# A fused two-layer convolution block: one xs store for each unit of layer 0, another buffer for a chunk of layer 1's results, three steps moved in the written order

## The chip, the core and the metric

The kernel runs on one core of a Trainium2 chip. It uses the core's five engines, named here as in the profile: PE (TensorE: matmuls, with its weight loads PEld), DVE (VectorE), ACT (ScalarE), POOL (GpSimd) and SP (SyncE, which here only issues DMAs), and 16 DMA engines. "ACTq" and "SPq" mark the DMAs and semaphore waits that ACT and SP take from their instruction queues. The metric is the device time of one execution in microseconds (us), the median of several.

## What is computed

Input x has 4 batches of 64 channels, 256 by 256, in float32. Two layers follow each other, each on a group-normalised input and with its input added:

```python
# --- layer 0 ---
h  = conv3x3(gn(x), c1_w) + c1_b
xa, k = split(conv1x1(h, c2_w) + c2_b, 2, axis=1)
xs = gelu(conv_vertical(conv_horizontal(xa, sh_w) + sh_b, sv_w) + sv_b)   # depthwise, 3 taps each
mask = top2(softmax(mean(xs, (2, 3)) @ gate_w.T))
out = xs
for i in range(3):                       # low ranks 2, 4, 8
    e = conv1x1(conv1x1(k, w2[i]) * conv1x1(xs, w1[i]), w3[i])
    out = out + e * mask[:, i]
x = x + conv1x1(out, proj_w)
# --- layer 1 ---
g = gn(x)
h = relu(batchnorm(conv3x3(g, quantize(w1))))
h = batchnorm(conv3x3(h, quantize(w2)))
x = x + relu(h + g)
```

The mean of xs over a whole batch is needed before any output of layer 0 of that batch; the group norm of layer 1 needs the whole batch of layer 0's result y; the batch norms need all four batches.

## The kernel before

**Tiles.** A batch is cut into 16 chunks of 16 image rows; a chunk of one tensor is a tile of 128 partitions by 2048 float32 (8 KB in each partition, 1 MB). Results that don't fit into the on-chip memory go to DRAM and come back: xs (`xs_d`), the low-rank products (`low_d`), y (`y_d`), layer 1's first convolution h1 (`h1_d`). Buffers are tags with a number of copies; a new tile of a tag waits until the tile that had its copy is no longer used by any engine or DMA, and this is tracked for a tile as a whole.

**Stages**, as the profile shows them: statistics of batch 0 (0 to 100 us); the "front" of layer 0, 64 units, one for each chunk of each batch (100 to 1262 us), with the outputs of the batch before and the statistics of the batch after mixed in; the boundary (about 1250 to 1340); conv1 of layer 1, 4 batches of 16 chunks (to about 1960), with the outputs of layer 0's last ten half-chunks of batch 2 and of all of batch 3 in between; conv2 (to about 2500); the last addition (to the end).

**The order** of instructions is written out by hand. Each call is placed with `at(step, order, ...)`; the calls are sorted by step and, within a step, by order, and all five engines keep to it: an engine works through its own instructions in this order, and different engines meet only at semaphores. So a call that is moved matters where it passes another call's instruction on the same engine's queue. Unit u of the front has two steps, 2u and 2u+1 (`at_slot(u, pos, ...)`: a position below 6 lies in the first, from 6 on in the second). conv1 begins at step 128 (`CONV1`), chunk k of batch b is around step 128 + 65 b + 4 k. The work of units 62 and 63 that would fall past step 127 is placed among conv1's first steps by a table `TAIL`.

**A unit of the front.** After the 3x3 convolution of a unit, each of its two halves (sub 0 and 1) passes the taps: PE (`front_taps_a`, `front_taps_b`, ps_a at L513), ACT (`front_taps_i`, t at L699), DVE (`front_taps_h`, t at L706, L714, L717), then ACT's Gelu into an xs tile (`front_xs`, L730). ACT's queue issues the store of that half (`xs_store`, L735, 0.5 MB, rows of 4 KB). The xs tag has 4 copies of a half. Once for every two units PE multiplies their four halves by the experts' first weights (`front_q`, L766), DVE forms the low-rank product (`front_low`, L771, tile k) and SP stores it (`low_store`, low_d<-k).

**The outputs of layer 0.** xs and the low-rank products come back (`xs_load`, `low_load`), x comes as the tile y (`out_load`, L835, y<-in_xp), PE projects (`out_open`, ps_o), DVE adds in place (`out_add`, L880), SP stores (`out_store`, L893, y_d<-y). In conv1's time these are placed by `plan_out_late`.

**A chunk of conv1.** SP loads y with one row of the chunk above (`conv1_load`, L912, yn<-y_d). POOL takes differences of rows, half by half, into a tile d (`conv1_differences`, the helper at L343). ACT normalises odd rows (`conv1_upper_odd`, L930 and L359) and makes the upper parts (`conv1_upper`, L346), DVE the lower parts (`conv1_lower`, L353, and `conv1_lower_odd`, L362), both into tiles that PE convolves (ps_hm, then ps_h for g = 0 and 1, L296, 12 matmuls each). ACT makes the part m that both halves share (`conv1_shared`, L312; for k of 2 and more in the single copy of the tag "k", that of the low-rank product). DVE combines ps_h and m into h1 (`conv1_out`, L318; two halves g). ACT squares for the statistics (`conv1_square`, L382) and its queue stores h1 (L998, h_d<-h, 1 MB). The h1 of odd chunks goes into the tile that held x of the front ("x", one copy, `chunk_x`), that of even ones into "h1" (one copy); in batch 0 chunk 1 goes into "h1" too.

Of the kernel before, what the change touches and what calls it, by code (L numbers as in the profile page):

```python
# [9 lines left out]
F32 = mybir.dt.float32  # L10
# [9 lines left out]
P = 128  # L20
# [6 lines left out]
GF = GP * W  # L27
# [14 lines left out]
def conv_preact_kernel(ctx: ExitStack, tc: tile.TileContext, io, col128, colset, col64):  # L42
# [130 lines left out]

    def weights():

        m64_t = work.tile([P, 2, GF], F32, tag="xs", name="m64", bufs=4)
        m64 = flat(m64_t)[0:C, 0 : io["m64"].shape[1]]
        n = io["mc1"].shape[1]
        taps = flat(work.tile([P, 2 * GP, W], F32, tag="t", name="taps", bufs=1))[:, 0:n]
        nc.sync.dma_start(taps, io["mc1"])  # L180
        nc.sync.dma_start(m64, io["m64"])
        nc.sync.dma_start(m128, io["m128"])

        def c64(name):
            return m64[:, col64[name][0] : col64[name][1]]

        front_weights(taps)
        n = 9 * C
        nc.vector.tensor_tensor(flat(av), taps[:, n : n + 3 * C], taps[:, n + 3 * C : n + 6 * C], ALU.mult)

        nc.vector.tensor_reduce(sv_sum, c128("sv"), AX.X, ALU.add)
        nc.vector.tensor_reduce(sh_sum, sh, AX.X, ALU.add)
        nc.vector.tensor_scalar(sh_bias, sh_sum, c128("c2_ba"), c128("sh_b"), ALU.mult, ALU.add)
        nc.vector.tensor_scalar(tap_bias, sv_sum, sh_bias, c128("sv_b"), ALU.mult, ALU.add)
        for i in range(2):
            nc.vector.tensor_scalar(end[:, i : i + 1], sh[:, 2 * i : 2 * i + 1], c128("c2_ba"), None, ALU.mult)
        nc.vector.tensor_scalar(ends, end, sv_sum, None, ALU.mult)
        nc.vector.tensor_scalar(edge_bias, ends, -1.0, tap_bias, ALU.mult, ALU.add)
        for i in range(2):
            o = outer[:, i, :]  # L200
            nc.vector.tensor_scalar(o, zeros[:, 0:W], sh_bias, None, ALU.add)
            nc.vector.tensor_tensor(o[:, 0 : W : W - 1], o[:, 0 : W : W - 1], end, ALU.subtract)
            nc.vector.tensor_scalar(o, o, c128("sv")[:, 2 * i : 2 * i + 1], None, ALU.mult)

        nc.vector.memset(wk, 0.0)
        ps = small("ps_wk")
        nc.tensor.matmul(ps[:, 0:NLOW], c64("c2_k"), c64("w2_t")[:, 0:NLOW], start=True, stop=True)

        for s in range(2):
            half = slice(s * C, s * C + C)  # L210
            for i in range(2):
                o = 16 * i
                nc.vector.tensor_copy(wk[half, s, i, o : o + NLOW], ps[half, 0:NLOW])
        ps = small("ps_kb")
        nc.tensor.matmul(ps[:, 0:1], c64("w2_t"), c64("c2_bk"), start=True, stop=True)
        nc.vector.tensor_tensor(k_bias, ps[:, 0:1], c128("e_b2"), ALU.add)
        ps = small("ps_pw3")
        nc.tensor.matmul(ps[:, 0:C], c64("w3"), c64("proj_t")[:, 0:C], start=True, stop=True)
        nc.vector.tensor_copy(pw3, ps[:, 0:C])
        ps = small("ps_pb3")  # L220
        nc.tensor.matmul(ps[:, 0:3], c64("proj_t"), c64("b3"), start=True, stop=True)
        nc.vector.tensor_copy(pb3, ps[:, 0:3])
# [503 lines left out]
    def front_xs(u, sub):  # L726
        b, k = divmod(u, NCH)
        n = 2 * k + sub
        x = xss[b, n] = work.tile([P, 2, GF], F32, tag="xs", name=f"xs_{b}_{n}", bufs=4)
        nc.scalar.activation(flat(x), flat(open_t.pop((u, sub))), AF.Gelu, accum_out=pooled[b][:, n : n + 1])  # L730

    def xs_store(u, sub):
        b, k = divmod(u, NCH)
        n = 2 * k + sub
        nc.scalar.dma_start(xs_d[b][:, n, :], flat(xss[b, n]))  # L735

    def front_k(b, j):

# [21 lines left out]
    def front_q(b, j):  # L760

        ps = ps_q[b, j] = bank("p", f"ps_q_{b}_{j}").rearrange("p s a b -> p s (a b)")
        for s in range(2):
            for i in range(4):
                x = xss[b, 4 * j + i][:, s]
                nc.tensor.matmul(ps[32 * i : 32 * i + 32, s], c128("e_w1"), x, start=True, stop=True)  # L766

    def front_low(b, j):
# [145 lines left out]
    def conv1_differences(b, k):  # L914

        y = y_in[b, k]
        if k == 0:
            nc.gpsimd.tensor_scalar(y[:, 0, :], zeros[:, 0:W], gn2[b][:, 0:1], None, ALU.add)
        if b == 0 and k < 4:
            both_raw = chunk_out(f"d_{b}_{k}", "o", 2)  # L920
        for n in range(2):
            if b == 0 and k < 4:
                raw_in[b, k, n] = both_raw[:, 4 * n : 4 * n + 4, :]
            else:
                raw_in[b, k, n] = work.tile([P, 4, W], F32, tag="xs", name=f"d_{b}_{k}_{n}", bufs=4)
            differences(first_rows(y)[n], raw_in[b, k, n], nc.gpsimd)

    def conv1_upper_odd(b, k):
# [38 lines left out]

    def conv1_out(b, k, g):
        if g == 0:
            if k % 2 and (b > 0 or k > 2):  # L970
                h_out[b, k] = flat(chunk_x(f"h1_{b}_{k}"))[:, 0 : CPAIR * W].rearrange("p (a b) -> p a b", b=W)
            else:
                h_out[b, k] = conv1_pool[0].tile([P, CPAIR, W], F32, tag="h1", name=f"h1_{b}_{k}", bufs=1)
        h = h_out[b, k]
        at_h = h[:, 4 * g : 4 * g + 4, :]
        first = k == g == 0
        total = sums[b][:, 2 * k + g : 2 * k + g + 1]
        leave(at_h, open_h.pop((b, k, g)), m_in[b, k][:, g], "w1", None if first else total)
        if first:
            nc.vector.tensor_reduce(total, h[:, 1:4, :], AX.XY, ALU.add)  # L980
            nc.vector.tensor_reduce(sums[b][0:C, NOCT : NOCT + 1], h[0:C, 0, :], AX.X, ALU.add)
            if b == 0:
                totals_less("h1", h[:, 1:3, :])
        if g:
            del m_in[b, k]
# [71 lines left out]
    def at_each(places, chain):  # L1057
# [6 lines left out]
    SLOTS = UNITS + 3  # L1064

    TAIL = {
# [6 lines left out]
    }  # L1073
# [9 lines left out]
    def plan_front():  # L1083
# [4 lines left out]
        for u in range(SLOTS):  # L1088
# [26 lines left out]
            if 0 <= u - 2 <= last:  # L1115
                at_slot(u, 2, front_taps_a, u - 2, 1)
                at_slot(u, 2.2, divide, u)
                at_slot(u, 4, front_taps_b, u - 2, 1)
                at_slot(u, 4.15, front_taps_i, u - 2, 1)
                at_slot(u, 5.2, front_taps_h, u - 2, 1)  # L1120
                at_slot(u, 5.3, front_xs, u - 2, 1)
                at_slot(u, 6.135, xs_store, u - 2, 1)
            if 0 <= u - 1 <= last:
                at_slot(u, 7, front_taps_a, u - 1, 0)
                at_slot(u, 7.2, divide, u)
                at_slot(u, 9, front_taps_b, u - 1, 0)
                at_slot(u, 9.1, front_taps_i, u - 1, 0)
                at_slot(u + 1, 1.15, front_taps_h, u - 1, 0)
                at_slot(u + 1, 1.55, front_xs, u - 1, 0)
                at_slot(u + 1, 1.6, xs_store, u - 1, 0)  # L1130
            j = (u - 2) // 2
            if u % 2 == 0 and 0 <= j < UNITS // 2:
                at_slot(u, 8, front_k, *divmod(j, NOCT // 4))
# [72 lines left out]
    def plan_out_late(b, ns, steps, order, end):  # L1206

        for n, step in zip(ns, steps):
            if n % 2 == 0:
                at(step - 9, 0.2, low_load, b, n // 2)  # L1210
                at(step - 9, 0.3, xs_load, b, n // 2, "h")
                at(step - 6, 0.4, out_load, b, n // 2)
            at(step, order, out_slot, b, n)
            if n % 2:
                at(step + 1, 13.3, out_store, b, n // 2)
        at_each(end, out_end(b))

    def conv1_first():
# [12 lines left out]
    def plan_conv1(b):  # L1231
# [4 lines left out]
        for k in range(NCH):  # L1236
# [11 lines left out]
            at(load, 0, conv1_load, b, k)  # L1248
            at(*late(diff, 13.08), conv1_differences, b, k)
            at(*late(odd, 13.36 if b == 0 and k == 3 else 13.1), conv1_upper_odd, b, k)  # L1250
            at(*late(up0, 13.12), conv1_upper, b, k, 0)
            at(*late(up1, 13.14), conv1_upper, b, k, 1)
            at(*late(low_odd, 13.2), conv1_lower_odd, b, k)
            at(*((t, 1.3) if first else late(low0, 13.22)), conv1_lower, b, k, 0)
            at(*((t, 1.32) if first else late(low1, 13.24)), conv1_lower, b, k, 1)
            at(T, 1.9 if first else 13, conv1_odd, b, k)
            at(T + 4 / 3, 13, conv1_even, b, k, 0)
# [377 lines left out]
```

## Time and profile before

| | us |
|---|---|
| median of 3 executions | 2971.59 (2965.42 to 2978.62) |
| the profiled execution | 2970.49 |
| its span | 2968.7 |
| PE, DVE, ACT, POOL busy | 2348.6, 2444.9, 2008.8, 1676.3 |
| ps_h, conv1's and conv2's matmuls (L296), busy | 756.5 |
| DVE's L318 waiting for the store of h1, longest | 12.7 |
| POOL's L343 waiting for the load of y, sum | 194.8, in 29 waits |
| SP waiting for DVE's L880 at the y store, sum | 492.2, in 64 waits |
| DMA, share of the 16 engines' time: SP's queue, ACT's queue | 71.3%, 11.3% |

Engines overlap, so their busy times add up to more than the span. The mean granted clock of PE was 0.916 of full speed, which includes the end without matmuls. Idle time is put down to the releaser that came last. An engine that waits is only a loss where the chain of work that ended last runs through it. The DMA share is the mean over 16 engines; GB/s count all bytes moved.

### The profile page before, as it was taken

Reading aid. Unit: us, or ns where it says so; the run is one execution under the profiler, and the core shown is the slowest. Engines: PE = TensorE matmul, PEld = TensorE weight load, DVE = VectorE, ACT = ScalarE, POOL = GpSimd, SP = SyncE. Lnnn points to the kernel's source line nnn. Section 1 sums busy time; section 2 is a strip of 40 time slices with the busy share of each in tenths; the row PEclk is TensorE's granted clock in tenths of the full one; section 3 lists DMA queues with packets and bytes.
Section 4 is the critical chain, followed back from the end, with each engine's and each line's share of the span. In section 5 each row is a group of like instructions: output and inputs, shape, how many; then the busy total and the mean of one; then the engine's idle time right before and its main releaser. Section 6 shows DMA issues by size and latency. Waiting matters only on the chain.

```text
span 2968.7 us, 52737 instructions
## 1 busy us (share of the span) xinstructions
PE 2348.6 (79%) x21576; PEld 1504.2 (51%) x21576; DVE 2444.9 (82%) x2811; ACT 2008.8 (68%) x2183; POOL 1676.3 (56%) x1252
## 2 busy tenths in 40 slices
PE   2888899999999999979999999989999999000000
PEld 1444445454445555546666667868788887000000
DVE  6688678888888988869988989979999898975664
ACT  4777887787876665557666668978888887432221
POOL 6988888787778888734544545735555564000000
PEclk9999999999999999989999999999999999555555
DMA  8665579999999999859999997747777764999999
GB/s 351 239 239 201 200 273 362 354 355 354 356 339 324 317 324 325 281 204 329 339 348 364 327 350 288 267 172 272 269 265 262 265 223 151 380 404 408 423 421 409
DMA packets 135715, 915.35 MB, mean 308 GB/s; under 512 B 14960, under 2 KB 15728, under 8 KB 40880
## 3 DMA queue, kind: packets, MB, share of 16 engines
q1 hardware_dynamic: 107824, 777.74, 71.3%
q10 hardware_dynamic: 27648, 134.23, 11.3%
q8 instruction: 170, 2.79, 0.4%
q14 instruction: 73, 0.60, 0.1%
HBM read 573.74 MB, written 338.17 MB: 307 GB/s over the span
## 4 chain that ended last, share of the span: by engine, by line
PE 51%; DMA 28%; DVE 12%; ACT 3%; issue 2%; POOL 2%; SPq 0%; ACTq 0%; DVEq 0%; POOLq 0%
PE ps_h L296 20%; PE ps_c L513 9%; DMA y<-in_xp 7%; PE ps_a L513 6%; PE ps_h2m L296 6%; DMA y_d<-y 5%; DMA y_end<-y_d 5%; PE ps_o L513 4%; DMA h<-h_d 4%; DMA out<-h 4%; PE ps_hm L296 4%; DVE t L714 1%; DVE t L717 1%; DMA yn<-y_d 1%; DMA xs_in<-in_xp 1%
## 5 line engine op out<-in xcount | busy, mean ns | idle before, releaser
L296 PE MATMUL ps_h<-diff,w_q 128*128 128x512 f32 x3072 | 756.5, 401 | 14.6 <-DVE h L318 14.2
L296 PEld LDWEIGHTS ps_h<-diff,w_q 128*128 128x128 f32 x3072 | 578.0, 190 | 194.2 <-issue 26.3
L513 PE MATMUL ps_c<-v,us 64*64 64x256 f32 x9216 | 535.2, 380 | 28.4 <-DVE ps_c L644 25.1
L343 POOL TENSOR_TENSOR d<-yn 128x1024 f32<-128x1024 f32 x128 | 346.2, 2724 | 305.9 <-DMA yn<-y_d 194.8
L513 PEld LDWEIGHTS ps_c<-v,us 64*64 64x64 f32 x9216 | 361.6, 134 | 175.5 <-issue 20.5
L343 POOL TENSOR_TENSOR d<-h 128x1024 f32<-128x1024 f32 x126 | 308.1, 2467 | 205.8 <-DVE diff L351 136.9
L513 PE MATMUL ps_a<-h,av 64*64 64x512 f32 x4080 | 386.1, 492 | 47.4 <-DVE t L717 40.8
L318 DVE SCALAR_TENSOR_TENSOR h<-ps_h,scale_w,m 128x1024 f32<-128x1024 f32 x256 | 323.1, 1279 | 78.0 <-PE ps_h L296 54.9
L561 POOL TENSOR_TENSOR x<-x 128x512 f32<-128x512 f32 x256 | 329.2, 1286 | 12.8
L1497 ACT ACTIVATE h<-h,shift,gn 128x2048 f32<-128x2048 f32 (+1 forms) x65 | 134.3, 2067 | 282.1 <-DVE h L1496 279.9
L513 PEld LDWEIGHTS ps_a<-h,av 64*64 64x64 f32 x4080 | 153.7, 133 | 321.0 <-issue 216.4
L382 ACT ACTIVATE junk<-h,less_h 128x2048 bf16<-128x2048 f32 (+3 forms) x134 | 256.3, 1912 | 13.6 <-DVE h L318 13.5
L1496 DVE SCALAR_TENSOR_TENSOR h<-h,inverse,y_end 128x2048 f32<-128x2048 f32 (+1 forms) x65 | 150.6, 2318 | 128.0 <-DMA y_end<-y_d 128.0
L699 ACT ACTIVATE t<-ps_a,tap_bias,m 128x1016 f32<-128x1016 f32 x128 | 153.5, 1199 | 118.4 <-PE ps_a L513 91.9
L880 DVE SCALAR_TENSOR_TENSOR y<-ps_o,ob,y 128x1024 f32<-128x1024 f32 x128 | 163.9, 1281 | 64.8 <-PE ps_o L513 26.1
L730 ACT ACTIVATE xs<-t 128x1024 f32<-128x1024 f32 x128 | 134.8, 1053 | 103.3 <-DVE t L717 89.5
L353 DVE SCALAR_TENSOR_TENSOR diff<-d,gn,diff 128x1024 fp32r<-128x1024 f32 x128 | 200.8, 1598 | 0.8 <-ACT diff L346 0.5
L296 PE MATMUL ps_h2m<-odd,w_q 128*128 128x512 f32 x768 | 193.5, 401 | 5.9 <-ACT odd L359 3.8
L296 PE MATMUL ps_hm<-odd,w_q 128*128 128x512 f32 x768 | 193.9, 402 | 2.8 <-DVE t L717 1.3
L346 ACT ACTIVATE diff<-d 128x1024 fp32r<-128x1024 f32 x128 | 135.2, 1056 | 82.2 <-POOL d L343 80.5
L553 POOL TENSOR_TENSOR x<-x,x 128x512 f32<-128x512 f32 x128 | 160.7, 1278 | 34.4 <-ACT x L547 34.3
L717 DVE SCALAR_TENSOR_TENSOR t<-ps_a,m,t 128x1020 f32<-128x1020 f32 x128 | 163.9, 1281 | 4.6
(256 smaller groups left out, 4237.1 us busy)
## 6 DMA issues: line engine op xcount, KB each, us to landing
x<-in_xc SPq DMA_DIRECT2D x64, 1280.0 KB
h<-h_d SPq DMA_DIRECT2D x64, 1152.0 KB
yn<-y_d SPq DMA_DIRECT2D x60, 1152.0 KB
xs_in<-in_xp SPq DMA_DIRECT2D x64, 1024.0 KB
xs_d<-xs ACTq DMA_DIRECT2D x128, 512.0 KB
xs_in<-xs_d SPq DMA_DIRECT2D x64, 1024.0 KB
y<-in_xp SPq DMA_DIRECT2D x64, 1024.0 KB
y_d<-y SPq DMA_DIRECT2D x64, 1024.0 KB
```

The costliest lines, as they stand in the source:

```text
L296: nc.tensor.matmul(ps, wq[w][:, kind, kx, :], t[:, rows, kx : kx + W], start=(j == 0), stop=(j == len(terms) - 1))
L318: nc.vector.scalar_tensor_tensor(h.rearrange("p (e k) w -> p e (k w)", e=2), ps.rearrange("p e k w -> p e (k w)"), w_scale[w], m.unsqueeze ...
L343: engine.tensor_tensor(raw.rearrange("p (g r) w -> p g r w", g=2), *pair, ALU.subtract)
L353: nc.vector.scalar_tensor_tensor(lower, raw, scale, upper.bitcast(F32), ALU.mult, ALU.subtract)
L382: nc.scalar.activation(junk[rows, 0:n], flat(h), AF.Square, bias=less[name][rows], accum_out=total)
L513: last[:] = [nc.tensor.matmul(ps[o, at_out[0] : at_out[1], :], w[i], rhs[i], **flags)]
L553: nc.gpsimd.tensor_tensor(x4[:, j - 1], x_rows(u, j + 2), x4[:, j - 1], ALU.subtract)
L561: nc.gpsimd.tensor_tensor(x[:, r : r + 2], x[:, r + 2 : r + 4], x[:, r : r + 2], ALU.subtract)
L699: nc.scalar.activation(t[:, :, inside], ps[:, :, inside], AF.Identity, bias=tap_bias, scale=sh[:, 1:2])
L717: nc.vector.scalar_tensor_tensor(t[:, :, 0 : W - 1], ps[:, :, 1:W], sh[:, 2:3], t[:, :, 0 : W - 1], ALU.mult, ALU.add)
L880: nc.vector.scalar_tensor_tensor(y, ps.rearrange("p x s w -> p x (s w)"), out_bias[b], y, ALU.add, ALU.add)
L1496: nc.vector.scalar_tensor_tensor(at_h, at_h, inverse[:, b : b + 1], y[:, a:e, :], ALU.mult, ALU.add)
```

## The change

It touches buffers and places in the order, in six edits.

1. **xs.** The tag "xs" has 2 copies of a whole unit (8 KB in a partition) in place of 4 of a half. Both halves are written into one tile, and one store of 1 MB (rows of 8 KB) for the unit is issued where that of the second half was, at the end of the slot two units on. `front_q` takes its halves from the unit's tile. The first weights' tile m64, which borrows the tag at the start, is shaped to it.
2. **Differences.** `conv1_differences` takes one tile of both halves for every chunk, from "o" (batch 0, k < 4) or "xs", in place of two half tiles for the later ones.
3. **h1 of batch 0's chunk 1** goes into "x".
4. **Chunk 1 of batch 0**: its two `conv1_upper` and the first `conv1_lower` move from 13.12, 13.14 and 13.22 to 13.36, 13.37 and 13.45 within their step, behind `front_taps_b` (13.2), `front_taps_i` (13.3) and, for the lower, `front_taps_h` (13.4) of the tail.
5. **`plan_out_late`**: `out_store` a step later.
6. **TAIL**: the entries of the store that is gone are gone.

```diff
@@ weights
-        m64_t = work.tile([P, 2, GF], F32, tag="xs", name="m64", bufs=4)
+        m64_t = work.tile([P, 4, GF], F32, tag="xs", name="m64", bufs=2)
@@ front_xs, xs_store
-        x = xss[b, n] = work.tile([P, 2, GF], F32, tag="xs", name=f"xs_{b}_{n}", bufs=4)
-        nc.scalar.activation(flat(x), flat(open_t.pop((u, sub))), AF.Gelu, accum_out=pooled[b][:, n : n + 1])
-
-    def xs_store(u, sub):
+        if sub == 0:
+            xss[u] = work.tile([P, 2, 2, GF], F32, tag="xs", name=f"xs_{u}", bufs=2)
+        x = xss[u][:, sub].rearrange("p s f -> p (s f)")
+        nc.scalar.activation(x, flat(open_t.pop((u, sub))), AF.Gelu, accum_out=pooled[b][:, n : n + 1])
+
+    def xs_store(u):
         b, k = divmod(u, NCH)
-        n = 2 * k + sub
-        nc.scalar.dma_start(xs_d[b][:, n, :], flat(xss[b, n]))
+        x = xss[u].rearrange("p n s f -> p (n s f)")
+        nc.scalar.dma_start(xs_d[b][:, 2 * k : 2 * k + 2, :].rearrange("p a b -> p (a b)"), x)
@@ front_q
-                x = xss[b, 4 * j + i][:, s]
+                x = xss[NCH * b + 2 * j + i // 2][:, i % 2, s]
@@ conv1_differences
-        if b == 0 and k < 4:
-            both_raw = chunk_out(f"d_{b}_{k}", "o", 2)
+        both_raw = chunk_out(f"d_{b}_{k}", "o" if b == 0 and k < 4 else "xs", 2)
         for n in range(2):
-            if b == 0 and k < 4:
-                raw_in[b, k, n] = both_raw[:, 4 * n : 4 * n + 4, :]
-            else:
-                raw_in[b, k, n] = work.tile([P, 4, W], F32, tag="xs", name=f"d_{b}_{k}_{n}", bufs=4)
+            raw_in[b, k, n] = both_raw[:, 4 * n : 4 * n + 4, :]
@@ conv1_out
-            if k % 2 and (b > 0 or k > 2):
+            if k % 2:
@@ TAIL
-        (0, 1.15): (0, 1.15), (0, 1.55): (0, 1.55), (0, 1.6): (0, 1.6), (0, 2): (0, 2), (0, 2.2): (0, 2.2),
+        (0, 1.15): (0, 1.15), (0, 1.55): (0, 1.55), (0, 2): (0, 2), (0, 2.2): (0, 2.2),
...
-        (1, 1.15): (3, 13.4), (1, 1.55): (3, 13.5), (1, 1.6): (4, 13.9), (1, 2): (5, 13.2), (1, 2.2): (5, 13.25),
+        (1, 1.15): (3, 13.4), (1, 1.55): (3, 13.5), (1, 2): (5, 13.2), (1, 2.2): (5, 13.25),
@@ plan_front
-                at_slot(u, 6.135, xs_store, u - 2, 1)
+                at_slot(u, 6.135, xs_store, u - 2)
...
-                at_slot(u + 1, 1.6, xs_store, u - 1, 0)
@@ plan_out_late
-                at(step + 1, 13.3, out_store, b, n // 2)
+                at(step + 2, 13.3, out_store, b, n // 2)
@@ plan_conv1
-            at(*late(up0, 13.12), conv1_upper, b, k, 0)
-            at(*late(up1, 13.14), conv1_upper, b, k, 1)
+            behind = b == 0 and k == 1
+            at(*late(up0, 13.36 if behind else 13.12), conv1_upper, b, k, 0)
+            at(*late(up1, 13.37 if behind else 13.14), conv1_upper, b, k, 1)
...
-            at(*((t, 1.3) if first else late(low0, 13.22)), conv1_lower, b, k, 0)
+            at(*((t, 1.3) if first else late(low0, 13.45 if behind else 13.22)), conv1_lower, b, k, 0)
```

## The prediction

> **What bounds the kernel now.** I read the page first, then busy time by stage, then the chain of waits in the stretches where TensorE (PE) falls short, then the neighbouring rows on each engine.
>
> ```profile
> PE 2348.6 (79%) x21576; PEld 1504.2 (51%) x21576; DVE 2444.9 (82%) x2811; ACT 2008.8 (68%) x2183; POOL 1676.3 (56%) x1252
> ...
> PE 51%; DMA 28%; DVE 12%; ACT 3%; issue 2%; POOL 2%; SPq 0%; ACTq 0%; DVEq 0%; POOLq 0%
> ```
>
> No engine is full, and the chain is half PE, over a quarter transfers. The stages tell which counts where (columns: stretch, its length, busy time of PE, PEld, DVE, ACT, POOL, granted PE clock, DMA share, GB/s):
>
> ```profile
> 500.00:700.00 200.00, 187.55 (x2628) 96.67 (x2624) 164.91 (x214) 155.15 (x218) 155.79 (x153) 1.00 0.97 353
> ...
> 1100.00:1250.00 150.00, 149.97 (x2136) 78.31 (x2136) 132.51 (x167) 87.12 (x110) 119.48 (x117) 1.00 0.89 310
> ...
> 1317.00:1333.00 16.00, 7.22 (x30) 5.29 (x29) 3.32 (x4) 7.46 (x7) 8.57 (x4) 0.82 0.99 351
> ...
> 1600.00:1700.00 100.00, 95.74 (x465) 65.17 (x464) 93.53 (x104) 67.55 (x68) 48.59 (x19) 0.97 0.93 336
> ```
>
> Layer 0's late units (1100 to 1250) are PE alone. Its middle, where results of the batch before go out (484 to 870), sits on transfers at 97%. At the boundary of the layers PE idles and its clock drops. The chain there:
>
> ```profile
> 1278.57 1.16 ACT diff L346
> ...
> 1282.82 1.29 DVE t L714
> ...
> 1285.57 3.92 PE ps_a L513 x24
> ...
> 1316.51 2.94 DMA low_d<-k
> ...
> 1319.53 0.08 ACT m L312
> 1319.61 11.58 DMA h_d<-h
> ...
> 1332.66 8.07 PE ps_h L296 x24
> ```
>
> Two things stand on it: a tap eviction queued behind upper parts (1278 to 1285), and the store of h1_0_1, 11.58 us, before PE moves at 1332.66.
>
> **Part 3, h1_0_1 in the place of x.** Now h1_0_2 needs the single "h1" buffer that h1_0_1's store still reads; the rows of DVE and of PE in the order of time name it (start, us, engine, operation, idle time before it).
>
> ```profile
> 1331.31 1.28 DVE L318 SCALAR_TENSOR_TENSOR h<-ps_h,scale_w,m 128x1024 f32<-128x1024 f32 x1 [12.68 <-DMA h_d<-h]
> ```
>
> ```profile
> 1332.66 8.07 PE L296 MATMUL ps_h<-diff,w_q 128*128 128x512 f32 x24 [8.78 <-DVE h L318]
> ```
>
> With the change h1_0_2 waits only for h1_0_0's store (issued 1304.88, landed by about 1310) and for m (L312, from 1319.53 to 1320.7). PE then runs on from 1323.88, so its 8.78 us go. The 24 matmuls after it took 8.07 us against 5.92 for the same 24 at 1314.94; the granted clock was 0.82 in the idle stretch, and if the idle made that, another 2.15 us go. What is late next: h1_0_3, also in "x", must wait for h1_0_1's store. That store is issued behind m, at about 1319.6 less part 4's 2 us, and by 11.6 us lands about 1329.2; DVE would be ready about 1328.6 and PE needs the bank about 1332.7, so 2 to 3 us of cover remain. If that store took 15 us the cover would be gone and each further us would cost one. Bounds: 0 (the same wait at h1_0_3) and −10.9. I take −10.5.
>
> **Part 4, upper and lower parts of chunk 1 behind the taps.** PE's taps of unit 62 end at 1279.2; ACT's L699 starts only at 1280.67, behind two L346 (2.20 us from 1278.57), and DVE's tap work at 1282.57, behind L353 (2.82 us from 1279.82). Behind them, L699 starts about 1279.3 and DVE ends about 1283.45 in place of 1285.4: −1.95 us, which PE's 3.36 us gap there can hand on. The moved steps issue two L346 on ACT and one 1024-wide L353 on DVE, no DMAs, and cross nothing of SP or POOL; they end about 3 us later, and PE first reads them at 1289.48, after L346 would end about 1283 and L353 about 1287. Cover 2 us. Bounds +1 and −2; I take −1.5.
>
> **Part 1, one xs store.** ACT's queue issues 64 DMAs fewer at 0.33 us each, mostly under running ACT work. What matters is a block: in every second unit of 484 to 870 the first half's store stands in front of the next L699 and leaves only when a y store lands.
>
> ```profile
> 550.51 14.42 DMA y_d<-y
> ...
> 565.00 0.34 ACTq L735
> ...
> 565.39 1.21 ACT t L699
> ...
> 590.54 14.12 DMA y_d<-y
> ...
> 604.73 20.28 DMA y<-in_xp
> ```
>
> I counted 11 such events, 1.2 to 3.7 us each, some 11 us together; PE's gaps behind L717 were 8.2 us in 500 to 700 and 8.1 in 700 to 900. The one store left comes at the end of the slot, where L699 isn't next. But the last rows belong to a loop of y store, y load and add (14.1, 20.3 and 5.4 us, the next y store at 630.36), about 40 us for two units at 97% DMA, so PE's idle there is mostly slack: a PE-bound unit takes 18.63 us (PE's starts at 1102.86 and 1121.48), these take 20.07, and the 28 us between come from the loop. The gain lies between all 11 us and, beyond nothing, a loss: rows of 8 KB took 309 ns median in the packet records, rows of 4 KB 159, so a y store whose 8 rows on each DMA engine alternate with the new store's can end 8 × 150 ns = 1.2 us later, 10 loops, +12. Since the bytes are the same and the load after it then runs freer, I take −3, bounds −11 and +12. The sole buffer wait that changes covers itself: a store now has some 27 us before unit u+2's L730 rewrites its buffer, against about 8 to land. The weights' first tile has the same bytes.
>
> The Trainium skill, "DMA: Bandwidth & Descriptors", section "Measured (HBM→SBUF, 128 partitions, SWDGE, issued from GpSimd)", asks for transfers of 1 MiB or more, and its rows of 1 MB and 64 KB suggest a fixed cost in each; it would favour this part, but the same page's "Queues, rings and completion order" has each engine take turns between the rings of queues, packet by packet, which speaks for the 1.2 us of the loop. The trace agrees with the first (0.5 MB about 8 us, 1 MB 9 to 11.6 in busy stretches); no row before shows the second. By the first the part could only gain; by the second the sum would end 12 us higher.
>
> **Part 5, y store one step later.** On SP it falls behind another DMA only in batch 2's conv1 (about 1603 to 1796), where a yn load now goes ahead of it.
>
> ```profile
> 1617.65 1.29 DVE y L880
> ...
> 1618.96 0.32 SPq L893
> ...
> 1619.45 17.62 DMA yn<-y_d
> ...
> 1637.23 5.77 POOL d L343 x2
> ```
>
> SP stood from 1608.61 to 1618.96 for the add, with the yn load behind, and POOL then waited for it; in 1600 to 1800 POOL waited 96.9 us in 16 such waits. The 17 chunks took 193 us, 11.35 each against 10.5 where PE alone sets them: 14 us to win at most, with DMA share 0.93, so not all. The moved load could stand in front of the store only if its buffer were not free, and that is free some 18 us before. Elsewhere the later y store passes nothing on SP or POOL, it only changes places with h1 stores on ACT's queue; its y buffer comes free a step (10.5 / 4 = 2.6 us) later, which the next y load, six steps ahead of its use, covers. Bounds −9 (seven early loads with about 1.3 us each) and +3; I take −5.
>
> **Part 2, one tile for both halves of the differences.** Its release is for the whole, so POOL's first half of chunk k waits for the second L353 of chunk k−2. The records show POOL's halves starting right behind L353, 3.6 to 4 us before that second one ends in 1336 to 1395. The first half ends 4.5 to 5.3 us before L930 reads it, so slack of 0.5 to 1.5 us is left; where yn is late nothing changes. For about 6 chunks DVE's L362 may then lie beside POOL's second half and lengthen by 0.2 to 0.5 us. Bounds 0 and +3; I take +1.
>
> Sum: −10.5 −1.5 −3 −5 +1 = −19, on the profiled 2970.49 us: 2951.5. The median, 2971.59, is 1.1 higher: 2952.
>
> **The rivals.**
> A, the wait moves. DMA was 0.99 busy while PE stood, and the chunks from 1407 to 1603 take 11.55 us, more than PE's 10.5: if transfers set that stage's end, layer 1 begins sooner and waits longer, or h1_0_3 inherits the wait. Against it: DMA falls to 0.32 to 0.4 at 1348 to 1356, so it isn't behind there. It keeps some 2 of the boundary's 12 us and half of the rest's 7: 2972 − 2 − 4 = about 2966.
> B, the stalls of the middle really set its pace: −11 there in place of −3 and −8 in batch 2: 2972 − 12 − 11 − 8 + 1 = about 2942. For it: L699 at 565.39 is on the chain. Against: 97% DMA.
> C, slower: the full 1 MB store beside the y store and y load lengthens their loop. Before, half a MB went beside each phase; the other half, 0.5 MB at 352 GB/s, is 1.5 us for each of 19 units, 28 us. For it: the loop is the chain and no share is left. Against: the bytes are the same, and delayed work is only reordered. 2972 − 12 − 5 + 1 + 28 = 2984, and 2987 with part 2's upper bound. It outweighs the rest from 16 us on, 0.85 us a unit.
> D, parts 1 and 5 don't do what they say: the one xs store waits as long and holds ACT at the slot's end, the yn load gains nothing because the bytes set its landing: 2972 − 12 + 1 = 2961.
>
> **How the numbers follow.** A difference of 0.5% (15 us) is about what a measurement of this kernel tells from no change: faster is below 2956.7, slower above 2986.4. My forecast has 0.40, B 0.15, A 0.18, D 0.12, C 0.15. The forecast's own range (bounds: boundary −4 to −13, middle ±6, batch 2 −8 to 0) is 2942 to 2962, three quarters of it below 2956.7. Faster: 0.30 + 0.15 + little of D and C = 0.48; slower: two thirds of C and a little of unknowns, 0.12; the rest, 0.40, is same. For 8 in 10 the range leaves out the lower half of B and most of C: 2936 to 2978.
>
> **What would show it.** Right: no wait of DVE's L318 for h_d<-h near 1331, PE without an 8.8 us gap there, the clock near 1; L699 directly behind PE at the taps of 62; in 484 to 870 no xs store leaving at the landing of a y store, units still about 20 us; fewer waits of POOL for yn in batch 2. Wrong: h1_0_3 waiting in place of h1_0_2 (A); units of 19 us in the middle (B); y stores of 15.5 us and more, units past 20.9 (C).

## The result, and the profile after

| | before | changed kernel |
|---|---|---|
| median, 22 executions each, same chip | 2971.22 us (2956.33 to 2985.95) | 2969.89 us (2963.41 to 2982.36) |
| ratio to before, 95% interval | | 0.9998 (0.9984 to 1.0011) |
| span of the profiled execution | 2968.7 us | 2968.1 us |

The time is the same. The page's busy times and the row of ACT's DMA queue (packets, MB, share of 16 engines) show what the change did as a whole:

```profile
PE 2345.5 (79%) x21576; PEld 1496.3 (50%) x21576; DVE 2452.3 (83%) x2811; ACT 2007.8 (68%) x2183; POOL 1660.0 (56%) x1252
...
q10 hardware_dynamic: 18432, 134.23, 11.1%
```

The same bytes in a third fewer packets (27,648 before), hardly less transfer time (11.3% before), and no engine with much less to do (the most is POOL, 16 us of 1676). Yet the stall that stood out in the profile is gone: rows of the changed kernel, PE's in the order of time and then DVE's (start, us, engine, operation, idle time before it), where PE had stood for 8.78 us.

```profile
1325.58 5.92 PE L296 MATMUL ps_h<-diff,w_q 128*128 128x512 f32 x24
1331.41 3.08 PE L296 MATMUL ps_hm<-odd,w_q 128*128 128x512 f32 x12
1334.33 5.82 PE L296 MATMUL ps_h<-diff,w_q 128*128 128x512 f32 x24
```

```profile
1331.39 1.28 DVE L318 SCALAR_TENSOR_TENSOR h<-ps_h,scale_w,m 128x1024 f32<-128x1024 f32 x1 [2.12 <-ACT m L312]
...
1341.76 1.28 DVE L318 SCALAR_TENSOR_TENSOR h<-ps_h,scale_w,m 128x1024 f32<-128x1024 f32 x1 [1.60 <-DMA h_d<-h]
```

PE runs through, its 24 matmuls take 5.82 us in place of 8.07, and DVE's first L318 of chunk 2 waits for m alone. The second row is h1_0_3, which now waits 1.60 us for h1_0_1's store. The stages, however (columns as before: stretch, length, PE, PEld, DVE, ACT, POOL, clock, DMA share, GB/s):

```profile
500.00:700.00 200.00, 182.60 (x2532) 91.89 (x2524) 158.89 (x205) 149.60 (x211) 151.96 (x149) 1.00 0.93 342
1100.00:1250.00 150.00, 149.48 (x2118) 77.18 (x2122) 131.72 (x167) 90.24 (x111) 123.16 (x119) 1.00 0.92 322
1327.00:1343.00 16.00, 16.00 (x70) 12.46 (x68) 10.54 (x14) 12.78 (x13) 12.03 (x6) 1.00 0.95 358
1600.00:1700.00 100.00, 95.03 (x466) 64.18 (x462) 92.47 (x104) 67.90 (x69) 46.78 (x20) 0.98 0.94 354
```

In 500 to 700 PE does 5 us less work than before and the DMA engines are idle more, 0.93 in place of 0.97. A shorter way to say it is to follow one instruction of each stage through both traces. The table gives how much later (+) or earlier (−), in us, it starts than in the profiled execution before: DVE's last tap of units 20, 40 and 60 (L717), its first L318 for chunks 2 and 9 of batch 0 and chunk 0 of batch 2, and for the first chunk of conv2; then the span. The experiments' rows are read below.

| kernel | u20 | u40 | u60 | chunk 2 | chunk 9 | batch 2 | conv2 | span |
|---|---|---|---|---|---|---|---|---|
| changed | 0.9 | 13.1 | 14.2 | 0.1 | 7.7 | 4.6 | 3.4 | −0.6 |
| e1 parts 3, 4 | 1.2 | −1.4 | −1.5 | −15.6 | −12.8 | −12.9 | −14.6 | −15.7 |
| e2 parts 1, 2 | 2.8 | 13.2 | 14.2 | 13.0 | 19.2 | 19.8 | 23.5 | 21.5 |
| e3 (as before) | 0.0 | −0.1 | −0.2 | 0.3 | 0.2 | −1.4 | −3.0 | −6.2 |
| e4 parts 3, 4, 5 | 0.5 | −2.5 | −2.6 | −16.6 | −13.9 | −12.3 | −18.0 | −5.3 |
| e5 late release | −0.4 | 8.5 | 8.5 | 7.2 | 13.4 | 15.8 | 14.0 | 9.9 |
| e6 two halves, late | 0.8 | 10.8 | 14.3 | −1.0 | 6.2 | 6.7 | 2.8 | 2.8 |
| e7 halves, old places | 0.1 | −4.1 | −4.1 | −19.6 | −12.0 | −15.2 | −16.3 | −22.7 |
| e8 store moved | 0.7 | −5.6 | −4.5 | −18.6 | −9.1 | −8.0 | −10.1 | −9.4 |
| e9 release by halves | 1.1 | 13.2 | 14.3 | 0.3 | 2.8 | 0.4 | −2.1 | −8.4 |
| e10 part 5 | 1.4 | −0.6 | −0.6 | −1.0 | −1.0 | −3.2 | −7.3 | −7.7 |
| e11 e8 and e9 | 2.1 | −2.9 | −1.8 | −15.8 | −12.4 | −10.3 | −14.1 | −11.3 |

The first row is the answer to where the time went: 12 us lost in units 20 to 40 (0.9 to 13.1), 14 won at the boundary (14.2 to 0.1), 7.6 lost by chunk 9, 4.3 won by conv2. The last stage moved the span by another −4 with the same instructions; the last section says how far that is chance.

### The profile page after: what moved, and what is told of

Read it like the earlier page. It is cut to its first block, busy times and chain, and to the rows that moved or that the text cites. A ratio compares the mean times of both kernels' runs of the same rounds, so it can differ in the third digit from the quotient of the medians.

```text
span 2968.1 us, 52675 instructions
## 1 busy us (share of the span) xinstructions
PE 2345.5 (79%) x21576; PEld 1496.3 (50%) x21576; DVE 2452.3 (83%) x2811; ACT 2007.8 (68%) x2183; POOL 1660.0 (56%) x1252
## 4 chain that ended last, share of the span: by engine, by line
PE 26%; DMA 23%; DVE 4%; POOL 1%; ACT 1%; issue 0%; SPq 0%; ACTq 0%; DVEq 0%; POOLq 0%
PE ps_h L296 17%; PE ps_h2m L296 6%; DMA y_end<-y_d 5%; DMA h<-h_d 4%; DMA out<-h 4%; DMA yn<-y_d 4%; DMA y<-in_xp 2%; DMA y_d<-y 2%; PE ps_hm L296 2%; DMA xs_in<-xs_d 2%; POOL d L343 1%; PE ps_o L513 1%; DVE diff L353 1%; DVE h L318 1%; DVE h L1494 1%; DVE h L1502 1%
## 5 line engine op out<-in xcount | busy, mean ns | idle before, releaser
L296 PE MATMUL ps_h<-diff,w_q 128*128 128x512 f32 x3072 | 754.5, 400 | 12.6 <-DVE h L318 12.4
L343 POOL TENSOR_TENSOR d<-yn 128x1024 f32<-128x1024 f32 x128 | 330.8, 2607 | 314.8 <-DMA yn<-y_d 173.8
L318 DVE SCALAR_TENSOR_TENSOR h<-ps_h,scale_w,m 128x1024 f32<-128x1024 f32 x256 | 323.1, 1279 | 62.3 <-PE ps_h L296 51.5
L561 POOL TENSOR_TENSOR x<-x 128x512 f32<-128x512 f32 x256 | 328.7, 1284 | 12.4
L699 ACT ACTIVATE t<-ps_a,tap_bias,m 128x1016 f32<-128x1016 f32 x128 | 153.4, 1199 | 120.9 <-PE ps_a L513 117.5
L353 DVE SCALAR_TENSOR_TENSOR diff<-d,gn,diff 128x1024 fp32r<-128x1024 f32 x128 | 204.5, 1628 | 0.0
L553 POOL TENSOR_TENSOR x<-x,x 128x512 f32<-128x512 f32 x128 | 160.5, 1275 | 34.0 <-ACT x L547 33.9
L717 DVE SCALAR_TENSOR_TENSOR t<-ps_a,m,t 128x1020 f32<-128x1020 f32 x128 | 163.9, 1280 | 4.6
```

The lines of the kernel that those rows point to most:

```text
L296: nc.tensor.matmul(ps, wq[w][:, kind, kx, :], t[:, rows, kx : kx + W], start=(j == 0), stop=(j == len(terms) - 1))
L318: nc.vector.scalar_tensor_tensor(h.rearrange("p (e k) w -> p e (k w)", e=2), ps.rearrange("p e k w -> p e (k w)"), w_scale[w], m.unsqueeze ...
L343: engine.tensor_tensor(raw.rearrange("p (g r) w -> p g r w", g=2), *pair, ALU.subtract)
L353: nc.vector.scalar_tensor_tensor(lower, raw, scale, upper.bitcast(F32), ALU.mult, ALU.subtract)
L553: nc.gpsimd.tensor_tensor(x4[:, j - 1], x_rows(u, j + 2), x4[:, j - 1], ALU.subtract)
L561: nc.gpsimd.tensor_tensor(x[:, r : r + 2], x[:, r + 2 : r + 4], x[:, r : r + 2], ALU.subtract)
```

## The experiments

Every time is a median against executions of before on the same chip, with the 95% interval of the ratio.

**e1, the boundary alone.** Before with

```diff
-            if k % 2 and (b > 0 or k > 2):
+            if k % 2:
...
+            behind = b == 0 and k == 1
...
+            at(*late(up0, 13.36 if behind else 13.12), conv1_upper, b, k, 0)
...
```

> Before with parts 3 and 4 alone (chunk 1 of h1 in the place of x, its upper and lower parts behind the taps). Theory 'sum of stages' (the boundary's gain is real and kept, the middle of layer 0 gave it back in the full change): the units up to 63 as before within 1 us, 13 to 14 us less by chunk 2 of batch 0, and the end 10 to 14 us earlier: about 2958. Rival 'absorbed' (transfers set layer 1's end, so what starts sooner waits longer): the same gain at chunk 2, but under 4 us of it left at the first conv2 chunk: about 2968 to 2971.

Measured: 2959.02 against 2969.43 us, 0.9963 (0.9947 to 0.9979). The gain at chunk 2, 14 us beside unit 60, is still there at conv2. In e1's PE rows the 24 matmuls that waited before run on:

```profile
1309.85 5.92 PE L296 MATMUL ps_h<-diff,w_q 128*128 128x512 f32 x24
1318.62 5.82 PE L296 MATMUL ps_h<-diff,w_q 128*128 128x512 f32 x24
```

The second began at 1332.66 before. Rival A of the prediction, absorption by the transfers of layer 1, falls.

**e2, the merged tiles alone.** Before with the hunks on m64, xs, `front_q`, differences and TAIL, in short:

```diff
-        x = xss[b, n] = work.tile([P, 2, GF], F32, tag="xs", name=f"xs_{b}_{n}", bufs=4)
+            xss[u] = work.tile([P, 2, 2, GF], F32, tag="xs", name=f"xs_{u}", bufs=2)
...
+        both_raw = chunk_out(f"d_{b}_{k}", "o" if b == 0 and k < 4 else "xs", 2)
...
-                at_slot(u + 1, 1.6, xs_store, u - 1, 0)
```

> Before with parts 1 and 2 alone (one xs tile and one store of 1 MB for a unit; one tile for both halves of the differences). 'Sum of stages': units 24 to 40 lengthen by 12 to 14 us together, conv1 of batch 0 by some 5 more, nothing comes back: about 2985 to 2990. Rival 'disturbed profile' (the 13 us in the middle were chance of one execution): units 24 to 40 within 3 us of before, time within 0.2%.

Measured: 2984.75 us, 1.0049 (1.0027 to 1.0071), slower. Units 20 to 40 lose 10.4 us and, counted from unit 16 on (+0.2), 13.0; chunk 2 to chunk 9 loses 6.2. What the changed kernel won at the boundary it lost by these two parts.

**e3, the release alone, first try.** The order in which the half tiles are taken is turned for every second pair of chunks.

```diff
-        for n in range(2):
+        for n in (0, 1) if k // 2 % 2 == 0 else (1, 0):
...
                 raw_in[b, k, n] = work.tile([P, 4, W], F32, tag="xs", name=f"d_{b}_{k}_{n}", bufs=4)
+        for n in range(2):
             differences(first_rows(y)[n], raw_in[b, k, n], nc.gpsimd)
```

> Before with the release of part 2 alone: the four half tiles stay, but are handed out so that POOL's first half of chunk k takes the tile of the second half of chunk k-2, and so waits for the same L353 as with one tile for both. If the wait for the second L353 costs what the full change lost between chunk 4 and chunk 9 of batch 0: 4 to 6 us later at chunk 9, and at the end by what the transfers leave of it, 0 to 6 us: 2971 to 2977. If the loss there came from the shifted transfers instead: within 1 us at chunk 9.

Measured: 2970.88 us, 0.9998 (0.9981 to 1.0016). It says nothing on the release: POOL's first halves still start 0.08 us behind the first L353. Its row serves as a second look at before: a difference of 3 us by conv2 comes without any change of the waits.

**e5, the release by force.** One small write to the second half's tile ahead of both halves.

```diff
+        if b or k > 3:
+            nc.gpsimd.memset(raw_in[b, k, 1][:, 0, 0:2], 0.0)
+        for n in range(2):
             differences(first_rows(y)[n], raw_in[b, k, n], nc.gpsimd)
```

> Before with the later release made by force: POOL first writes two columns of the second half's tile and so waits for the second L353 of chunk k-2 before either half, for every chunk that has half tiles. (e3 did not change the waits: which buffer a tile gets followed the order of first use, and its trace shows POOL starting 0.08 us behind the first L353 as before.) If this release is what e2 lost behind chunk 2: POOL's two halves back to back behind the second L353, chunks 4 to 9 of batch 0 some 6 us later together, 4 to 10 us at the start of conv2. If e2's loss there came from its transfers lying otherwise: under 2 us at chunk 9.

Measured: 2980.64 against 2971.50 us, 1.0044 (1.0028 to 1.0059), slower. Chunk 2 to 9 loses 6.2 us, as in e2. Its rows show how. POOL's two halves stand behind the second L353 and run back to back, and an instruction of the gate on DVE (the top-2 mask of batch 3) that starts beside them ends with them:

```profile
1357.16 4.74 POOL L343 TENSOR_TENSOR d<-yn 128x1024 f32<-128x1024 f32 x2 [3.62 <-DVE diff L353]
```

```profile
1359.63 2.29 DVE L809 TENSOR_TENSOR beat<-gate 128x3 f32<-128x3 f32 x1
```

In the trace before, the same instruction is

```profile
1352.18 0.16 DVE L809 TENSOR_TENSOR beat<-gate 128x3 f32<-128x3 f32 x1
```

From chunk 2 to 9 three such instructions (L809, L814, L831) took 2.27 to 2.36 us each, 0.15 to 0.16 before, and two of the 14 L353 took 3.43 us in place of 1.28.

The 8.9 us that this execution lost in units 20 to 40 aren't explained: no instruction there is changed, and yet a y store left only every 20.7 us (20.0 before). So a single profile of that stretch can mislead. Whether the other four executions (all five lie at 2979.0 to 2984.7 us) lost there too isn't known.

**e9, the release undone.** The changed kernel with one lasting tile, of which xs and the differences take parts, so that each half waits for itself.

```diff
-            xss[u] = work.tile([P, 2, 2, GF], F32, tag="xs", name=f"xs_{u}", bufs=2)
+            xss[u] = xs_all[0][:, 4 * (u % 2) : 4 * (u % 2) + 4, :].rearrange("p (n s) f -> p n s f", n=2)
...
+                i = 4 * (k % 2) + 2 * n
+                raw_in[b, k, n] = flat(xs_all[0][:, i : i + 2, :]).rearrange("p (a b) -> p a b", b=W)
```

> The changed kernel with part 2 undone in its effect: xs and the differences live in parts of one lasting tile, so that POOL waits for each half alone, as before; the one store of 1 MB stays where the change put it. If part 2's release costs what e2 and e5 showed behind chunk 2: chunk 9 of batch 0 at before's cadence (no loss from chunk 4 on), the time 5 to 10 us under the changed kernel's: 2960 to 2966. If part 2 costs nothing in the full change: 2968 to 2972.

Measured: 2964.41 against 2973.97 us, 0.9987 (0.9967 to 1.0006). That is where it was expected, but its interval overlaps the changed kernel's (0.9984 to 1.0011), so the gain is seen in the traces alone. At the table's marks up to chunk 2 it is the changed kernel within 0.3 us, and from there it loses 2.5 us to chunk 9 in place of 7.6. What the release does is seen in POOL's rows, first of the changed kernel, then of e9:

```profile
1340.24 4.74 POOL L343 TENSOR_TENSOR d<-yn 128x1024 f32<-128x1024 f32 x2 [3.97 <-DVE diff L353]
1352.32 4.73 POOL L343 TENSOR_TENSOR d<-yn 128x1024 f32<-128x1024 f32 x2 [7.34 <-DVE diff L353]
```

```profile
1348.57 2.42 POOL L345 TENSOR_TENSOR xs_all<-yn 128x1024 f32<-128x1024 f32 x1 [3.64 <-DVE diff L355]
1352.27 2.40 POOL L345 TENSOR_TENSOR xs_all<-yn 128x1024 f32<-128x1024 f32 x1 [1.28 <-DVE diff L355]
```

In the changed kernel both halves run back to back; in e9, at this moment, one by one, 3.7 us apart, each behind its L355 (the changed kernel's L353). And DVE's rows at that moment, first of the changed kernel, then of e9:

```profile
1354.78 2.29 DVE L811 TENSOR_TENSOR beat<-gate 128x3 f32<-128x3 f32 x1
1356.99 1.27 DVE L318 SCALAR_TENSOR_TENSOR h<-ps_h,scale_w,m 128x1024 f32<-128x1024 f32 x1
```

```profile
1354.74 0.16 DVE L813 TENSOR_TENSOR beat<-gate 128x3 f32<-128x3 f32 x1
1354.82 1.28 DVE L320 SCALAR_TENSOR_TENSOR h<-ps_h,scale_w,m 128x1024 f32<-128x1024 f32 x1
```

The same three elements a partition take 2.29 us beside POOL's second half, which ends at 1352.32 + 4.73 = 1357.05, and 0.16 us without it. The next L318, which frees PE's bank, comes 2.2 us later. L833, one element, does the same later (2.33 against 0.15 us). There it reaches PE, which has no gap above 0.6 us from 1336 to 1412 in the trace before:

```profile
1382.61 4.63 PE L296 MATMUL ps_h<-diff,w_q 128*128 128x512 f32 x12 [2.26 <-DVE h L318]
```

These 12 matmuls also took 4.63 us (24 took 5.93 in e9), at a granted clock of 0.85 in 1376 to 1386. From chunk 7 to chunk 8 PE's first ps_hm matmul falls back 4.8 us in the changed kernel and not at all in e9.

Not all of this is the release. The pair of halves that held L833 waited last for a late yn load:

```profile
1376.42 4.91 POOL L343 TENSOR_TENSOR d<-yn 128x1024 f32<-128x1024 f32 x2 [1.88 <-DMA yn<-y_d]
```

e9 has such a pair at 1375.41, but there the same instruction had run just before it, at 1375.34. So the release explains the first hold; that the second followed from DVE being late is argued from these rows, not shown. The Trainium skill, "SBUF — State Buffer", section "SBUF: two separate sides", says that VectorE and GpSimd share one pair of ports as an exclusive lock for a whole instruction, where the VectorE instruction has two inputs in SBUF, as these have, and the GpSimd one reads SBUF; the rows agree, to the end of POOL's instruction.

**e6, two halves in the new place; e7, two halves in the old places; e8, the one store moved.** All three are the changed kernel with other stores (in e7 and e8 with the entries of `TAIL` to match):

```diff
 e6
-        nc.scalar.dma_start(xs_d[b][:, 2 * k : 2 * k + 2, :].rearrange("p a b -> p (a b)"), x)
+        for n in range(2):
+            nc.scalar.dma_start(xs_d[b][:, 2 * k + n, :], xss[u][:, n].rearrange("p s f -> p (s f)"))
 e7
+                at_slot(u, 6.135, xs_store, u - 2, 1)
...
+                at_slot(u + 1, 1.6, xs_store, u - 1, 0)
 e8
-                at_slot(u, 6.135, xs_store, u - 2)
+                at_slot(u + 1, 1.6, xs_store, u - 2)
```

> The changed kernel with the unit's xs as two stores of 0.5 MB (rows of 4 KB), both issued at the one place at the end of the slot. Theory 'place' (1 MB of xs beside the y store delays it, whatever its rows): units 24 to 40 lengthen by 11 to 15 us as in the changed kernel, time within 3 us of 2970. Rival 'rows' (rows of 8 KB take longer turns against the y store's): at most 4 us there, time 2958 to 2962.

> The changed kernel with two stores of 0.5 MB from the merged tile, each in the place it had before. By 'place' and by 'rows' alike units 24 to 40 go back to before's within 2 us: time 2956 to 2960, since part 2 still costs. Should they still lengthen by over 5 us, the merged tile itself (its release for the whole) is the cause and not the store.

> The changed kernel with its one store of 1 MB half a slot later, in the place where the first half of the next unit was stored before (ahead of L699, away from the y store's issue). 'Place': the loss in units 24 to 40 falls to under 5 us and the time to 2958 to 2963, unless the store now blocks L699 as the first half's did. 'Rows': the loss stays above 9 us, since the same rows then lie beside the y load and the rest of the y store.

Measured against 2971.50 us: e6 2971.99, 0.9998 (0.9977 to 1.0020); e7 2955.95, 0.9947 (0.9921 to 0.9974); e8 2956.69, 0.9958 (0.9942 to 0.9974). 1 MB at the end of the slot costs 12 to 15 us (0.9998 against 0.9958 and 0.9947) whether in one store or in two, in rows of 8 KB or of 4; the same 1 MB in one store half a slot later costs nothing. It is the place, not the rows and not the number of DMAs. The table sorts the same way: from unit 20 to 40 the four executions with 1 MB in that place (changed, e2, e6, e9) lose 10.1 to 12.2 us, and the others lose nothing (up to 6.3 us are won), but for e5. The waits of 548 to 866 (engine, line, waited for: us in total, times, longest), of before, of the changed kernel, of e6 and of e8:

```profile
DVE y L880 <- DMA y<-in_xp: 12.1, 8, 2.7
```

```profile
DVE y L882 <- DMA y<-in_xp: 16.6, 4, 5.4
...
PE ps_o L513 <- DVE y L882: 12.9, 8, 2.2
```

```profile
DVE y L882 <- DMA y<-in_xp: 18.5, 5, 5.2
```

```profile
DVE y L882 <- DMA y<-in_xp: 10.4, 5, 2.8
```

From the issues and landings in 540 to 860, a mean of 15 to 16 each: before, a y load took 17.0 us and a y store 15.9; in the changed kernel 18.3 and 16.9; in e6 17.8 and 16.1; in e7 17.0 and 15.8; in e8 17.2 and 15.1. The y stores follow each other every 20.0 us before, 20.8 in the changed kernel and e6, 19.9 in e7, 19.8 in e8. The 1 MB leaves 1.4 us after a y store in the changed kernel, two halves leave 1.3 and 1.8 us after it in e6; before and in e7 one half leaves 1.4 us after it and the other 10 to 15, in e8 the 1 MB 9 to 16. How the place lengthens the loop is not fully shown: e6 has the changed kernel's pace with 33.9 us for load and store together, the changed kernel 35.2, and the unexplained profile of e5, with its halves in the old places, 34.2.

**e10, part 5 alone.**

```diff
-                at(step + 1, 13.3, out_store, b, n // 2)
+                at(step + 2, 13.3, out_store, b, n // 2)
```

> Before with part 5 alone (y store a step later). Forecast of the prediction: 5 us less (0 to 9), won between chunk 0 of batch 2 and chunk 0 of batch 3; nothing before. Rival 'bytes set the landing': within 1.5 us there, time within 0.15% of before.

Measured: 2968.23 against 2973.97 us, 0.9986 (0.9967 to 1.0005). The order is as meant, in SP's rows of e10:

```profile
1609.32 0.52 SPq L912 DMA_DIRECT2D yn<-y_d  x1
1618.36 0.32 SPq L893 DMA_DIRECT2D y_d<-y  x1
```

The yn load leaves 9 us ahead of the y store, where before it followed it at 1619.45. POOL's waits for yn in 1600 to 1800 fall from 96.9 to 75.3 us, and from batch 2 to conv2 the trace gains 4.1 us (−3.2 to −7.3). The median points the same way but its interval holds no change. In the table the same stretch falls by 1.2 to 5.7 us in the eight executions with part 5 (3.0 in the mean) and moves by −1.7 to +3.7 in the four others (e1, e2, e3, e5).

**e4 and e11, better versions.** e4 is before with parts 3, 4 and 5 and neither merged tile; e11 is the changed kernel with e8's place and e9's tile.

> Before with parts 3, 4 and 5 (no merged tiles). 'Sum of stages': e1's gain at chunk 2, and in batch 2 of conv1 3 to 6 us more from the later y store: about 2953 to 2956. 'Absorbed': 2966 to 2971. Should part 5 bring nothing, the time is e1's within 2 us.

> e8 (the store half a slot later) together with e9 (release by halves), parts 3, 4 and 5 as in the change. 'Sum of stages': e8's gain in units 24 to 40, no loss from chunk 4 on: 2946 to 2953, below before and the changed kernel. If e8's release wait was hidden: e8's time, 2955 to 2958.

Measured: e4 2953.91 against 2969.43 us, 0.9942 (0.9919 to 0.9965); e11 2951.17 against 2973.97 us, 0.9936 (0.9912 to 0.9960). Both are faster than before and than the changed kernel; which of the two is faster is open.

## Why the prediction was wrong

It forecast 2952 us and a gain clear of noise; 2969.9 lies in its range but is no change. The gain at the boundary that it named is real; part 1 had the wrong sign and part 2's cost was taken too small.

- **Part 3**, forecast −10.5: right. DVE's first L318 of chunk 2 moved by −10.6 against that of chunk 1 in the changed kernel and in e1, and PE's matmuls by −11.2 from chunk 2 to chunk 4. What was to be late next came too: h1_0_3's wait in "x", 1.60 us. It moved DVE's first L318 of chunk 3 by 1.9 us (0.1 to 2.0; e1: −15.6 to −13.7), but PE kept what it had won (−16.2 in e1 still at chunk 9), so the cover that had been counted held.
- **Part 4**, forecast −1.5, bound −2: measured −3.6 (14.2 at unit 60 to 10.6 at the last tap of unit 63, and −1.5 to −5.1 in e1). PE's row of the taps, before and in the changed kernel:

```profile
1285.57 3.92 PE L513 MATMUL ps_a<-h,av 64*64 64x512 f32 x24 [3.36 <-DVE t L717]
```

```profile
1297.85 2.38 PE L513 MATMUL ps_a<-h,av 64*64 64x512 f32 x24 [1.37 <-DVE t L717]
```

  The gap fell by 1.99 us, the 1.95 that were worked out. The term left out that the 24 matmuls behind it ran faster too, 2.38 us in place of 3.92, at a granted clock of 1.00 (1297.8 to 1300.2) in place of 0.60 (1285.5 to 1289.5). Part 3 had counted the same for its own gap.
- **Part 5**, forecast −5: e10 agrees in size with 4.1 us in the trace and 0.14% (4 us) in the median, though not beyond its interval. e4 against e1 (0.9942 and 0.9963) points the same way, with overlapping intervals.
- **Part 2**, forecast +1, bound +3: it cost 5.1 us at DVE's chunk 9 (7.6 against 2.5 in e9; 6.2 in e2 and e5). The step that failed: "For about 6 chunks DVE's L362 may then lie beside POOL's second half and lengthen by 0.2 to 0.5 us." The overlap was named, but its price was that of a slowed instruction and on the wrong line: L362 took the same in e5 as before (8.5 us for 7), while gate instructions and L353 that started behind POOL were held until it ended, some 2.1 us each time.
- **Part 1**, forecast −3: it cost 12 us (from unit 16 on 12.3 in the changed kernel and 13.0 in e2; 12 to 15 by the medians of e8 and e7). The step that failed: "Since the bytes are the same and the load after it then runs freer, I take −3". The load didn't run freer: it took 18.3 us in place of 17.0, the y store 16.9 in place of 15.9. What happened is nearest to rival C at under half its price (0.6 us for a unit over units 20 to 40, not 1.5): the whole MB behind the y store's start lengthens the loop, and the bytes being the same didn't matter. The bound by rows (1.2 us for each y store, +12) met the size by luck, for e6 shows that rows aren't the cause. What the stalls in front of L699 were worth alone no run shows: the fast kernels have a store in that place (e7, e8), and those without have the whole MB beside the y store.

The rivals: A's 2966 is the nearest number, but by luck, for e1 kept its gain to the end. B fell (units of 20.8 us, not 19). C's sign, y stores of 15.5 us and more, could not tell anything, since they took 15.9 us already before; its upper figure sums to 2986, not 2987, and the forecast's own sum is 2952.6.

From e4, −17 us by the median (0.9942), and e2, +15 (1.0049), the sum is −2; the changed kernel measured −1.

## What to carry to other kernels

Where a chain of store, load and add through DRAM sets the pace at 97% DMA share, ask of every transfer what it lies beside: here 1 MB moved by half a slot was worth 12 us, in two halves apart 15, its packing into one DMA nothing. When tiles are merged to save DMAs, look for everything else that takes the tag, and what the coarser release does to the rhythm of engines that get in each other's way. Price such an overlap by the whole instruction that holds the other, not by a few per cent.

## What was not expected of the hardware

- A VectorE instruction on three elements a partition took 2.29 us behind a GpSimd TENSOR_TENSOR, 0.16 us without it.
- The pace of units 20 to 40 can differ between executions though no instruction there is changed: e5 stood at +8.5 us by unit 40, e3 and e10 at −0.1 and −0.6. So part 1's 12 us rest on four executions with 1 MB in that place (10.8 to 13.2 by unit 40) and on the medians of e6, e7 and e8, not on one profile.
- The last stage, transfers alone, took 439 to 458 us in the 13 profiled executions (span less the last L318 of conv2: 458 in e4, 439 in e7 and e9, 445 before, 441 after), with the same instructions. A difference of spans below some 10 us between single executions of this kernel tells nothing.
